# Latent attention with ternary experts: attention moved by a chunk, and the experts' input transposed through DRAM in the last five blocks

## The chip, the cores and the metric

The kernel runs on one core of a Trainium2 chip. The metric is the device time in microseconds (us) of one launch, taken as the median of three runs. One execution was also profiled; its instruction records are the trace that this document reads. The engines are called by their names or as the profile calls them: PE is TensorE (matmuls), PEld its weight loads, DVE is VectorE, ACT is ScalarE, POOL is GpSimd, SP is SyncE, whose queue issues every DMA of this kernel.

## The reference

The input is 4096 tokens of width 512. All is fp32. For each token:

```python
h = layernorm(x)
Q, V = h @ Wq.T + bq, h @ Wv.T + bv           # 16 heads of 32
logits = Q . latent / sqrt(32)                # 64 latent keys per head
w = softmax(top_4(logits))                    # the other 60 weigh nothing
attn = sum(w * latent) + V
x = x + layernorm(attn @ Wo.T + bo)
h = layernorm(x)
up, gate = h @ wu, h @ wg                     # 512 -> 2048, ternary weights
x = x + layernorm((silu(up) * gate) @ wd)     # 2048 -> 512, ternary weights
```

A ternary weight is `clip(round(W / s), -1, 1) * s` with `s = mean(|W|)`. The same latent vectors are keys and values.

## The kernel before

The tokens are cut into 8 blocks of 512 (`NB`, `TB`), a block into 4 row tiles of 128 tokens (`TT`), the width into 4 column tiles (`DC`). Each block goes through attention and then through the experts. The order is written by hand (`manual_schedule`): within one engine, instructions run in the order in which the code emits them, and an instruction waits only for the results and buffers that it needs from other engines, DMAs or its own predecessors.

**The experts** of a block (`class Experts`) run in 16 chunks `e` of 128 hidden columns. A chunk emits `up("u")`, tanh (ACT), `silu` (DVE), `up("g")`, `gate` (DVE), `high` (ACT), `down(e - 1)`, `low` (DVE). Each of `up("u")`, `up("g")` and `down` is 8 matmuls of 128x512, because every activation is split into a high part (rounded to fp32r) and a low part (the rest), and both are multiplied. The PSUM banks of `pu` and `pg` exist once each: `up("u", e + 1)` waits until `silu(e)` has read `pu`, `up("g", e + 1)` until `gate(e)` has read `pg`, and `down(e)`, which is emitted in chunk `e + 1`, needs the high and the low part of chunk `e`. The first matmul of a block reads the high part of all four row tiles, the second the low part.

**The attention** of block b+1 is emitted in pieces between the chunks of block b. The function `pieces` is the list of places: `put(e, k, f, ...)` puts a step into chunk `e` at place `k`. Place 3 is ahead of tanh; place 0 is between tanh and `silu`; place 1 between `up("g")` and `gate`; place 2 behind `down(e - 1)` and ahead of `low`. The steps are, for the attention block `A`:

- `q(c)`: queries of four heads (PE), copied by ACT. `l(c)`: logits (PE), copied by ACT into two tiles `w`. The hidden rows are read as `taken(k)` or `ordered(k)`, two orders of the same transposed tile `hT`.
- `m(i)`, `r(i)`, `e(i)`, `n(i)`, `z(i)` for eight groups of heads: the four largest (DVE), the marking of them (DVE), exponentials (ACT), normalisation (DVE), and a transpose of the weights that is done as a transpose of 32x32 blocks on DVE, a write to DRAM (`dz`), and four loads back (`wT`).
- `v(c)`, `y(c)`: values and the weighted latents in one bank (PE), copied by ACT into `attnT`. The first two `v` use the bank of `pg` (`gate_psum`), the others one of the two banks `at`.
- `o(t)`, `o_bias(t)`: the output projection of a row tile (8 matmul instructions on PE), bias and statistics (DVE). `o_rstd` (POOL), `o_apply(t)`: layer norm (DVE) and the addition to x (POOL).
- `f_stats`, `f_rstd`, `f_apply(t)`: the experts' layer norm; `f_trans(t)`: four transposes of 128x128 on PE into a bank `at`, from which ACT copies the high part `hT_f` and DVE subtracts the low part `lT_f`.

**The next attention block's input** (`after`, two blocks ahead) is loaded by `load_normed` in chunk 6 as four row tiles `xa`, normalised in place (`a_stats`, `a_rstd`, `a_apply`), transposed by `a_blocks` in 32x32 blocks on DVE, one column tile at a time (16 instructions of 128x128), written to DRAM (`da`), and read back by `a_load` into `hT`. `hT` of block b+2 shares its buffer with `hT_f` of block b, so that `a_load` waits for the last gate matmul of the block. Blocks 0 and 1 (`FirstAttention`) and 2 (`SecondAttention`) make `hT` by transposes on PE; block 0's attention is ordered by the string `FIRST_STEPS`.

In before, the places behind the output projection of an attention block are:

```python
put(11, 2, A.o, 0, range(DC), gate_psum)      # and o_bias(0), o(1) to o(3), o_rstd(0, 2)
put(12, 1, A.o_rstd, 2, 4)
put(12, 2, A.o_apply, 0)                      # and 1;  2 and 3 at (13, 0)
put(13, 1, A.f_stats, 0)                      # and 1, f_rstd(0, 2);  2, 3, f_rstd(2, 4) at (13, 2)
put(14, 0, A.f_apply, 0)                      # and 1;  2 and 3 at (14, 1)
put(14, 1, A.f_trans, 0)                      # and 1;  2 and 3 at (15, 0)
```

The functions that the diff touches, and what calls them, with the line numbers of the profile:

Of the kernel before, what the change touches and what calls it, by code (L numbers as in the profile page):

```python
# [10 lines left out]
F32 = mybir.dt.float32  # L11
F32R = mybir.dt.float32r
BF16 = mybir.dt.bfloat16
AF = mybir.ActivationFunctionType
ALU = mybir.AluOpType
AX = mybir.AxisListType

P = 128
# [40 lines left out]
def latent_attention_ternary_glu(  # L59
# [15 lines left out]
    nc = tc.nc  # L75
    NT, D = x_in.shape
    E = wuT.shape[1]
    DC = D // P
    EC = E // P
    TB = 512  # L80
    TT = TB // P
# [5 lines left out]
    work = ctx.enter_context(tc.tile_pool(name="work", bufs=2))  # L87
    small = ctx.enter_context(tc.tile_pool(name="small", bufs=4))
    dram = ctx.enter_context(tc.tile_pool(name="dram", bufs=3, space=bass.MemoryType.DRAM))
# [20 lines left out]
    def transposed(which, b, name, dtype):  # L110
        return work.tile([P, DC, TB], dtype, tag=f"{which}{b % 2}", name=name, bufs=1)
# [7 lines left out]
    CH = E // 2  # L119
    halves = [(k, h) for k in range(DC) for h in range(2)]  # L120
    raw = {}
    late = []
    for q in range(DC):
        w = work.tile([P, D], F32, tag="xa", name=f"raw_d_6_{q}", bufs=TT)
        late.append(w)
    for n, i in RAW_ORDER:
        raw[n, i] = wpool.tile([P, CH], F32, tag="chunk", name=f"raw_{n}_{i}", bufs=6 * DC)
    for q in range(DC):
        raw["d", 6 + q] = late[q]
    count = {"u": 2 * DC, "g": 2 * DC, "d": 2 * DC + 2}  # L130

    def load_x(b):
# [8 lines left out]
    normed = {}  # L141

    def load_normed(b):
        for t in range(TT):
            xt = work.tile([P, D], F32, tag="xa", name=f"xa_{b}_{t}", bufs=TT)
            r = b * TB + t * P
            nc.sync.dma_start(out=xt, in_=x_in[r : r + P, :])
            normed[b, t] = xt

    def load_up(n, src):  # L150
        for i, (k, h) in enumerate(halves):
# [46 lines left out]
    tern = {}  # L198
# [84 lines left out]
    def transpose_row(h, name):  # L283
        pt = at_psum(f"pt_{name}")
        for c in range(DC):
            nc.tensor.transpose(pt[:, c * P : (c + 1) * P], h[:, c * P : (c + 1) * P], ident)  # L286
        return pt.rearrange("p (c k) -> p c k", k=P)
# [3 lines left out]
    class Attention:  # L291
        def __init__(self, b):
            self.b = b
            self.hT = None
            self.attnT = None
            self.norm_a = Norm(f"a{b}")
            self.norm_o = Norm(f"o{b}")
            self.norm_f = Norm(f"f{b}")
            self.rows = {}
            self.qT, self.w, self.top, self.m8, self.left, self.wT, self.pv = ({} for _ in range(7))  # L300
            self.po = {}

        def a_stats(self, t):
            self.norm_a.stats(t, normed[self.b, t])

        def a_rstd(self, lo, hi):
            self.norm_a.rstd(lo, hi)  # L310

        def a_apply(self, t):
            self.norm_a.apply(normed[self.b, t], normed[self.b, t], t)

        def a_blocks(self, c):

            if c == 0:
                self.da = dram.tile([P, 4, DC, P], F32, tag="da", name=f"da_{self.b}", bufs=2)
            z = work.tile([P, 4, P], F32, tag="w", name=f"za_{self.b}_{c}", bufs=4)
            for t in range(TT):  # L320
                nc.vector.transpose(
                    z[:, :, 32 * t : 32 * t + 32],
                    normed[self.b, t][:, c * P : (c + 1) * P].rearrange("p (k j) -> p k j", j=32),
                )
            nc.sync.dma_start(out=self.da[:, :, c, :], in_=z)

        def a_load(self):
            self.hT = transposed("X", self.b, f"hT_{self.b}", F32)
            for k in range(4):
                nc.sync.dma_start(  # L330
                    out=self.hT[32 * k : 32 * k + 32, :, :],
                    in_=self.da.rearrange("(a j) k c e -> k j a (c e)", j=32)[k],
                )

        def taken(self, k):
            return self.hT.rearrange("p a (c e) -> p c a e", e=P)[:, k]

        def ordered(self, k):  # L340
            return self.hT.rearrange("p a (c t i) -> p c t a i", t=TT, i=32)[:, k]


        def q(self, c):
# [145 lines left out]
            self.rows["f", t] = row(f"h_f{self.b}_{t}")  # L490
            self.norm_f.apply(self.rows["f", t], x_tiles[self.b][t], t)

        def f_alloc(self):
            self.hi = transposed("X", self.b, f"hT_f{self.b}", F32R)
            self.lo = transposed("Y", self.b, f"lT_f{self.b}", F32R)

        def f_trans(self, t):
            src = transpose_row(self.rows.pop(("f", t)), f"f{self.b}_{t}")
            dst = self.hi[:, :, t * P : (t + 1) * P]
            nc.scalar.copy(dst, src)  # L500
            nc.vector.tensor_tensor(
                self.lo[:, :, t * P : (t + 1) * P], src, dst.bitcast(F32), ALU.subtract
            )

    class SecondAttention(Attention):
# [9 lines left out]
        def sorted(self, dst, src):  # L517
            return self.mixed(dst), src.rearrange("p (a t i) -> p a t i", t=TT, i=32)

        def a_apply(self, t):  # L520
            self.rows["a", t] = row(f"h_a{self.b}_{t}")
            self.norm_a.apply(self.rows["a", t], normed[self.b, t], t)

        def a_trans(self, t):
            if self.hT is None:
# [143 lines left out]
    class Experts:  # L669
# [6 lines left out]
        def up(self, n, e):  # L676
            p = ps_up.tile([P, TB], F32, tag=n, name=f"p{n}_{self.b}_{e}")
            for k in range(DC):
                for i, part in enumerate(self.parts):
                    nc.tensor.matmul(  # L680
                        p, lhsT=tern[n, 2 * k + e // 8][:, (e % 8) * P : (e % 8 + 1) * P], rhs=part[:, k, :],
                        start=(k == 0 and i == 0), stop=(k == DC - 1 and i == 1),
                    )
            (self.pu if n == "u" else self.pg)[e] = p
# [91 lines left out]
    A = FirstAttention(0)  # L776
# [105 lines left out]
    def pieces(A, after):  # L882

        at = {(e, k): [] for e in range(EC) for k in range(4)}

        def put(e, k, f, *args):
            at[e, k].append(lambda: f(*args))

        if A.b > 1:
            if A.b == 2:  # L890
                put(0, 0, A.a_apply, 0)
                put(0, 0, A.a_apply, 1)
                put(0, 1, A.a_trans, 0)
                put(0, 1, A.a_trans, 1)
                put(0, 1, A.a_apply, 2)
                put(0, 1, A.a_apply, 3)
                put(0, 2, A.a_trans, 2)
                put(0, 2, A.a_trans, 3)
            put(1, 0, A.q, 0)
            put(2, 0, A.q, 1)  # L900
            put(4, 0, A.q, 2)
            put(6, 0, A.q, 3)
        put(1, 1, A.l, 0)
        put(2, 2, A.l, 1)
        for i in range(8):
            put(2 + i, 0, A.m, i)
            put(2 + i, 2, A.r, i)
            put(3 + i, 3, A.e, i)
            put(3 + i, 1, A.n, i)
            put(3 + i, 1, A.z, i)  # L910
        for c in range(2):
            put(5 + 2 * c, 0, A.v, c, gate_psum)
            put(5 + 2 * c, 0, A.y, c)
            put(5 + 2 * c, 0, A.l, c + 2)
        for c in range(2, DC):
            put(5 + 2 * c, 1, A.v, c)
            put(5 + 2 * c, 1, A.y, c)
        if after is not None and after.b == 2:
            put(14, 2, after.a_stats, 0)
            put(14, 2, after.a_stats, 1)  # L920
            put(15, 1, after.a_stats, 2)
            put(15, 1, after.a_stats, 3)
            put(15, 1, after.a_rstd, 0, 4)
        elif after is not None:
            put(10, 2, after.a_stats, 0)
            put(10, 2, after.a_stats, 1)
            put(11, 0, after.a_stats, 2)
            put(11, 0, after.a_stats, 3)
            put(11, 0, after.a_rstd, 0, TT)
            for t in range(TT):  # L930
                put(11, 1, after.a_apply, t)
            for c in range(DC):
                put(11, 2, after.a_blocks, c)
            put(15, 2, after.a_load)
        put(11, 2, A.o, 0, range(DC), gate_psum)
        put(11, 2, A.o_bias, 0)
        for t in range(1, TT):
            put(11, 2, A.o, t)
            put(11, 2, A.o_bias, t)
        put(11, 2, A.o_rstd, 0, 2)  # L940
        put(12, 1, A.o_rstd, 2, 4)
        put(12, 2, A.o_apply, 0)
        put(12, 2, A.o_apply, 1)
        put(13, 0, A.o_apply, 2)
        put(13, 0, A.o_apply, 3)
        put(13, 1, A.f_stats, 0)
        put(13, 1, A.f_stats, 1)
        put(13, 1, A.f_rstd, 0, 2)
        put(13, 2, A.f_stats, 2)
        put(13, 2, A.f_stats, 3)  # L950
        put(13, 2, A.f_rstd, 2, 4)
        put(14, 0, A.f_apply, 0)
        put(14, 0, A.f_apply, 1)
        put(14, 1, A.f_alloc)
        put(14, 1, A.f_trans, 0)
        put(14, 1, A.f_trans, 1)
        put(14, 1, A.f_apply, 2)
        put(14, 1, A.f_apply, 3)
        put(15, 0, A.f_trans, 2)
        put(15, 0, A.f_trans, 3)  # L960
        return at

    prev = None
    for b in range(NB):
        if b > 0:
            A, nxt = nxt, after
        after = None
        F = Experts(b, (A.hi, A.lo))
        at = {}
        for e in range(EC):  # L970
            if e == 4 and 0 < b < NB - 1:
# [119 lines left out]
```

## Time and profile before

| | |
|---|---|
| median of 3 runs | 1169.82 us (1168.61 to 1170.22) |
| profiled execution | 1169.52 us |
| its span, first to last instruction | 1167.3 us |
| PE, DVE, ACT, POOL busy | 1145.6, 853.1, 371.9, 172.7 us |
| granted TensorE clock, mean | 0.998 |
| PE transposes of the experts' input, `pt_f`, 8 blocks | 128 instructions, 17.3 us |
| share of pt_f in the chain that ended last | 1.1% |
| block-transposed weights written to DRAM, `dz` | 56 DMAs, 256 KB each, 2.0 us to landing |
| block-transposed rows written, `da`, and read, `hT` | 20 and 20 DMAs, 256 KB each, 2.9 and 5.1 us to landing |

The time of the profiled execution exceeds its span by 2.2 us, which lie before the first and behind the last recorded instruction. A duration in the profile is that of one instruction; instructions of one engine overlap a little, so the distance from start to start is shorter (a matmul of 128x512 is 390 ns long, and one starts every 227 ns). The chain of waits gives what each stretch of work adds to the end. An instruction's idle time stands in brackets behind it, with what ended it.

### The profile page before, as it was taken

The page shows a single profiled execution, that of the slowest core. Times are in us where ns is not written, and L with a number is a line of the kernel's source. Part 1 is how long each engine was busy: PE and PEld are TensorE (multiplying, and loading weights), DVE is VectorE, ACT ScalarE, POOL GpSimd, SP SyncE. Part 2 cuts the span into 40 slices and gives each one's busy share as a digit, 9 for nine tenths or more (in the row PEclk, how much of TensorE's full clock was granted, in tenths as well). Part 3 has the DMA queues.
Part 4 walks back from the last instruction along what each step waited for, and adds up shares of the span by engine and source line. Part 5 has one row for each costly group of instructions (what it writes and reads, how often), then busy time and mean ns, then how long its engine had stood idle before and what let it go on. Part 6 is the DMA issues. An engine that isn't in the chain of part 4 may idle for free.

```text
span 1167.3 us, 14552 instructions
## 1 busy us (share of the span) xinstructions
PE 1145.6 (98%) x4730; PEld 784.6 (67%) x4730; DVE 853.1 (73%) x2981; ACT 371.9 (32%) x654; POOL 172.7 (15%) x205
## 2 busy tenths in 40 slices
PE   8999999999999999999999999999999999999997
PEld 5446665866757766676766766577665866757885
DVE  5975884968867779777787688776886868847435
ACT  4984441333312332133321232122331233312222
POOL 1066000320023000320003200032000320013100
PEclk9999999999999999999999999999999999999999
DMA  9700121013111231122220232201412112100000
GB/s 353 287 1 1 63 65 54 1 53 129 64 45 37 99 98 56 37 73 75 89 85 6 73 103 78 72 19 54 136 56 63 37 52 93 64 10 1 37 1 36
DMA packets 73323, 80.38 MB, mean 69 GB/s; under 512 B 7200, under 2 KB 46368, under 8 KB 73248
## 3 DMA queue, kind: packets, MB, share of 16 engines
q1 hardware_dynamic: 73248, 79.46, 20.9%
q8 instruction: 37, 0.61, 0.2%
q14 instruction: 38, 0.31, 0.1%
HBM read 51.12 MB, written 28.31 MB: 68 GB/s over the span
## 4 chain that ended last, share of the span: by engine, by line
PE 91%; DVE 6%; ACT 1%; DMA 1%; issue 1%; POOL 0%; SPq 0%; DVEq 0%
PE pg L680 20%; PE pu L680 19%; PE acc L723 19%; PE po L463 8%; PE pv L435 8%; PE pq L348 7%; PE pv L452 3%; PE pl L362 3%; PE pq L553 2%; DVE left L388 1%; PE pt_f L286 1%; DVE m L380 1%; PE po L636 1%; DVE w L408 1%; DVE w L390 0%
## 5 line engine op out<-in xcount | busy, mean ns | idle before, releaser
L680 PE MATMUL pg<-hT_f,tern_g 128*128 128x512 f32 x512 | 211.4, 413 | 0.8 <-ACT attnT L442 0.8
L723 PE MATMUL acc<-tern_d,hi 128*128 128x512 f32 x512 | 202.9, 396 | 1.7 <-DVE y L276 1.7
L680 PE MATMUL pu<-hT_f,tern_u 128*128 128x512 f32 x512 | 203.3, 397 | 0.7 <-ACT hT_f L657 0.7
L723 PE MATMUL acc<-tern_d,lo 128*128 128x512 f32 x512 | 199.8, 390 | 0.1
L680 PE MATMUL pu<-lT_f,tern_u 128*128 128x512 f32 x512 | 199.5, 390 | 0.2 <-DVE lT_f L663 0.2
L680 PE MATMUL pg<-lT_f,tern_g 128*128 128x512 f32 x512 | 199.6, 390 | 0.0
L708 ACT CAST hi<-h 128x512 fp32r<-128x512 f32 x128 | 79.4, 620 | 263.9 <-DVE h L697 263.8
L689 ACT ACTIVATE h<-pu,columns 128x512 f32<-128x512 f32 x128 | 87.2, 681 | 216.1 <-PE pu L680 215.4
L697 DVE TENSOR_TENSOR h<-h,pg 128x512 f32<-128x512 f32 x128 | 86.2, 673 | 85.4 <-PE pg L680 84.7
L692 DVE SCALAR_TENSOR_TENSOR h<-h,pu 128x512 f32<-128x512 f32 x128 | 86.1, 673 | 67.7 <-ACT h L689 67.7
L723 PEld LDWEIGHTS acc<-tern_d,hi 128*128 128x128 f32 x512 | 96.1, 188 | 34.5 <-issue 13.4
L713 DVE TENSOR_TENSOR lo<-h,hi 128x512 fp32r<-128x512 f32 x128 | 93.7, 732 | 34.9 <-ACT hi L708 34.9
L680 PEld LDWEIGHTS pg<-hT_f,tern_g 128*128 128x128 f32 x512 | 96.1, 188 | 27.1 <-issue 4.1
L680 PEld LDWEIGHTS pg<-lT_f,tern_g 128*128 128x128 f32 x512 | 96.2, 188 | 24.3 <-issue 5.7
L680 PEld LDWEIGHTS pu<-hT_f,tern_u 128*128 128x128 f32 x512 | 96.1, 188 | 23.5 <-issue 1.7
L680 PEld LDWEIGHTS pu<-lT_f,tern_u 128*128 128x128 f32 x512 | 96.1, 188 | 21.7 <-issue 1.7
L723 PEld LDWEIGHTS acc<-tern_d,lo 128*128 128x128 f32 x512 | 96.2, 188 | 19.9 <-DVE lo L713 0.9
L435 PE MATMUL pv<-hT,wv 128*128 128x512 f32 x224 | 100.7, 592 | 0.8 <-DVE h L697 0.8
L388 DVE MATCH_REPLACE8 left<-m,w 128x64 f32<-128x64 f32 x512 | 100.3, 211 | 0.0
L463 PE MATMUL po<-wo,attnT 128*128 128x512 f32 x224 | 97.3, 592 | 0.0
L348 PE MATMUL pq<-hT,wq 128*128 128x512 f32 x192 | 86.2, 592 | 0.0
L463 PEld LDWEIGHTS po<-wo,attnT 128*128 128x128 f32 x224 | 42.5, 190 | 50.8 <-issue 48.6
(130 smaller groups left out, 1327.2 us busy)
## 6 DMA issues: line engine op xcount, KB each, us to landing
dz<-z SPq DMA_DIRECT2D x56, 256.0 KB, 2.0
wT<-dz SPq DMA_DIRECT2D x224, 64.0 KB, 1.9
x<-in_x SPq DMA_DIRECT2D x32, 256.0 KB, 3.8
out_x<-x SPq DMA_DIRECT2D x31, 256.0 KB, 2.0
xa<-in_x SPq DMA_DIRECT2D x24, 256.0 KB, 3.5
da<-za SPq DMA_DIRECT2D x20, 256.0 KB, 2.9
hT<-da SPq DMA_DIRECT2D x20, 256.0 KB, 5.1
raw_u<-in_wuT SPq DMA_DIRECT2D x8, 512.0 KB, 8.4
```

What stands on the lines that cost most here:

```text
L348: nc.tensor.matmul(pq, lhsT=wq[:, k, c * P : (c + 1) * P], rhs=self.taken(k), start=(k == 0), stop=(k == DC - 1),)
L362: nc.tensor.matmul(pls[pr][:, t * P : (t + 1) * P], lhsT=qT[rows, t * P : (t + 1) * P], rhs=lk[rows, c, :], start=True, stop=True, tile_po ...
L388: nc.vector.match_replace(left[:, g, :], m8[:, g, :], w[:, g, :], TAKEN)
L435: nc.tensor.matmul(self.pv[c], lhsT=wv[:, k, c * P : (c + 1) * P], rhs=self.ordered(k), start=(k == 0), stop=False,)
L463: nc.tensor.matmul(self.po[t], lhsT=self.attnT[:, c, t * P : (t + 1) * P], rhs=wo[:, c, :], start=(c == 0), stop=(c == DC - 1),)
L680: nc.tensor.matmul(p, lhsT=tern[n, 2 * k + e // 8][:, (e % 8) * P : (e % 8 + 1) * P], rhs=part[:, k, :], start=(k == 0 and i == 0), stop=( ...
L689: nc.scalar.activation(self.h[e], self.pu[e], AF.Tanh, scale=half_u[0])
L692: nc.vector.scalar_tensor_tensor(self.h[e], self.h[e], 1.0, self.pu.pop(e), ALU.add, ALU.mult)
L697: nc.vector.tensor_tensor(self.h[e], self.h[e], self.pg.pop(e), ALU.mult)
L708: nc.scalar.copy(hi, self.h[e])
L713: nc.vector.tensor_tensor(lo, self.h.pop(e), self.hid[e][0].bitcast(F32), ALU.subtract)
L723: nc.tensor.matmul(self.acc[t], lhsT=part[:, t * P : (t + 1) * P], rhs=wd, start=(e == 0 and i == 0), stop=(e == EC - 1 and i == 1),)
```

## The change

Attention blocks 3 to 7 (the five for which `A.b > 2`) get an offset `s = 1`: all their steps from `l` to the output projection move to one chunk earlier, `q` to (0, 2), (1, 1), (3, 0), (5, 0), `m(0)` to (1, 1). Behind the output projection, which is now at (10, 2), the layer norms stand closer together, and `f_trans` gives way to three new steps: `f_blocks(t)` transposes a normalised row tile in 32x32 blocks (one DVE instruction of 128x512) and writes it to DRAM; `f_load(half)` reads two row tiles back with four DMAs; `f_split(t)` copies the high part (ACT) and subtracts the low part (DVE). The tile `whole` that is read back takes the place of the normalised rows `xa`, which become one tile of four row tiles, loaded with one DMA. `a_blocks` now takes one row tile at a time (4 instructions of 128x512 in place of 16 of 128x128), and `taken` and `ordered` read the order that results. For block 1, whose pieces run in block 0, the first two `v` and `y` go to place 1, behind `l`, and into a bank `at`. `f_trans` stays for blocks 1 and 2.

```diff
     def load_normed(b):
-        for t in range(TT):
-            xt = work.tile([P, D], F32, tag="xa", name=f"xa_{b}_{t}", bufs=TT)
-            r = b * TB + t * P
-            nc.sync.dma_start(out=xt, in_=x_in[r : r + P, :])
-            normed[b, t] = xt
+        normed[b] = work.tile([P, TT, D], F32, tag="xa", name=f"xa_{b}", bufs=1)
+        nc.sync.dma_start(
+            out=normed[b], in_=x_in[b * TB : (b + 1) * TB, :].rearrange("(t p) d -> p t d", p=P)
+        )
...
-        def a_blocks(self, c):
...
+        def blocks(self, which, t, h):
+            if t == 0:
+                self.far[which] = dram.tile(
+                    [P, 4, TT, P], F32, tag="far", name=f"far_{which}{self.b}", bufs=3
+                )
+            z = work.tile([P, 4, P], F32, tag="w", name=f"z{which}_{self.b}_{t}", bufs=4)
+            nc.vector.transpose(
+                z.rearrange("p k (c i) -> p c k i", i=32),
+                h.rearrange("p (c k j) -> p c k j", k=4, j=32),
             )
+            nc.sync.dma_start(out=self.far[which][:, :, t, :], in_=z)
+
+        def a_blocks(self, t):
+            self.blocks("a", t, normed[self.b][:, t, :])
...
         def taken(self, k):
-            return self.hT.rearrange("p a (c e) -> p c a e", e=P)[:, k]
+            return self.hT.rearrange("p a (t c i) -> p c a t i", t=TT, i=32)[:, k]
 
         def ordered(self, k):
-            return self.hT.rearrange("p a (c t i) -> p c t a i", t=TT, i=32)[:, k]
+            return self.hT.rearrange("p a (t c i) -> p c t a i", t=TT, i=32)[:, k]
...
+        def f_blocks(self, t):
+            self.blocks("f", t, self.rows.pop(("f", t)))
+
+        def f_load(self, half):
+            if half == 0:
+                self.whole = work.tile([P, 4, TB], F32, tag="xa", name=f"hw_{self.b}", bufs=1)
+            part = slice(2 * half * P, (2 * half + 2) * P)
+            for k in range(4):
+                nc.sync.dma_start(
+                    out=self.whole[32 * k : 32 * k + 32, :, part],
+                    in_=self.far["f"].rearrange("(a j) k t e -> k j a (t e)", j=32)[k][:, :, part],
+                )
+
+        def f_split(self, t):
...
+            src = self.whole[:, :, t * P : (t + 1) * P].rearrange("p a (c i) -> p c a i", i=32)
...
+            nc.scalar.copy(hi, src)
+            nc.vector.tensor_tensor(lo, src, hi.bitcast(F32), ALU.subtract)
...
+        s = 1 if A.b > 2 else 0
...
+        elif A.b > 2:
+            put(0, 2, A.q, 0)
+            put(1, 1, A.q, 1)
+            put(3, 0, A.q, 2)
+            put(5, 0, A.q, 3)
...
         for c in range(2):
-            put(5 + 2 * c, 0, A.v, c, gate_psum)
-            put(5 + 2 * c, 0, A.y, c)
-            put(5 + 2 * c, 0, A.l, c + 2)
+            if A.b > 1:
+                put(5 - s + 2 * c, 0, A.v, c, gate_psum)
+                put(5 - s + 2 * c, 0, A.y, c)
+            put(5 - s + 2 * c, 0, A.l, c + 2)
+            if A.b == 1:
+                put(5 + 2 * c, 1, A.v, c)
+                put(5 + 2 * c, 1, A.y, c)
...
-        put(11, 2, A.o_rstd, 0, 2)
...
+        put(11 - s, 2, A.o_rstd, 0, 2)
+        if s:
+            put(10, 2, A.o_rstd, 2, 4)
+            put(11, 0, A.o_apply, 0)
+            put(11, 0, A.o_apply, 1)
+            put(11, 1, A.o_apply, 2)
+            put(11, 1, A.o_apply, 3)
+            put(11, 2, A.f_stats, 0)
+            put(11, 2, A.f_stats, 1)
+            put(11, 2, A.f_rstd, 0, 2)
+            put(12, 0, A.f_stats, 2)
+            put(12, 0, A.f_stats, 3)
+            put(12, 0, A.f_rstd, 2, 4)
+            for t in range(TT):
+                put(12, 1 + t // 2, A.f_apply, t)
+                put(12, 1 + t // 2, A.f_blocks, t)
+            put(12, 2, A.f_load, 0)
+            put(13, 0, A.f_load, 1)
+            for t in range(TT):
+                put(14 + (t + 2) // 3, (t + 2) % 3, A.f_split, t)
```

## The prediction

> **What bounds the kernel now.** I read the page's busy shares first, then the chain by engine.
>
> ```profile
> PE 1145.6 (98%) x4730; PEld 784.6 (67%) x4730; DVE 853.1 (73%) x2981; ACT 371.9 (32%) x654; POOL 172.7 (15%) x205
> PE 91%; DVE 6%; ACT 1%; DMA 1%; issue 1%; POOL 0%; SPq 0%; DVEq 0%
> ```
>
> TensorE is busy 98% and carries 91% of the chain; VectorE's 73% is an average. A block lasts 140 us (output projections start at 609.15, 749.11, 889.67). So I read the chain in order of time where the change works, behind the output projection (start, length):
>
> ```profile
> 749.11 13.73 PE po L463 x32
> 762.85 1.83 PE pu L680 x8
> 764.67 1.81 PE pg L680 x8
> 766.49 1.81 PE acc L723 x8
> ...
> 777.37 0.87 PE pt_f L286 x8
> 778.25 1.83 PE acc L723 x8
> 780.07 1.82 PE pu L680 x8
> 781.89 0.87 PE pt_f L286 x8
> 782.76 1.84 PE pg L680 x8
> ```
>
> No gap: a chunk is three groups of eight matmuls, 1.815 us each. The projection is already one piece (32 matmuls together), and the transposes are two pieces of 0.87 us. How near VectorE is to TensorE here shows in its timeline:
>
> ```profile
> 764.44 0.66 DVE L713 TENSOR_TENSOR lo<-h,hi 128x512 fp32r<-128x512 f32 x1
> 765.49 0.69 DVE L692 SCALAR_TENSOR_TENSOR h<-h,pu 128x512 f32<-128x512 f32 x1 [0.40 <-ACT h L689]
> 766.52 0.69 DVE L697 TENSOR_TENSOR h<-h,pg 128x512 f32<-128x512 f32 x1 [0.35 <-PE pg L680]
> 767.13 1.00 DVE L276 TENSOR_SCALAR o<-o,mv_o,rs_o 128x512 f32<-128x512 f32 x2
> 768.65 2.95 DVE L276 TENSOR_SCALAR o<-o,mv_o,rs_o 128x512 f32<-128x512 f32 x2
> ...
> 775.91 0.66 DVE L713 TENSOR_TENSOR lo<-h,hi 128x512 fp32r<-128x512 f32 x1
> 776.49 1.00 DVE L276 TENSOR_SCALAR h_f<-x,mv_f,rs_f 128x512 f32<-128x512 f32 x2
> ```
>
> From 764.44 to 776.57 VectorE is idle for 0.40 + 0.35 us only. Its last product there, `lo` of chunk 13, is needed by `down` at 778.25: 1.7 us to spare. Two groups price what is added:
>
> ```profile
> L415 DVE STREAM_TRANSPOSE z<-w 128x512 f32<-128x512 f32 x56 | 39.8, 711 | 1.9
> L276 DVE TENSOR_SCALAR h_f<-x,mv_f,rs_f 128x512 f32<-128x512 f32 x32 | 17.3, 578 | 0.0
> ```
>
> And block 0, chunk 5, has TensorE's real waits:
>
> ```profile
> 126.05 3.70 PE L435 MATMUL pv<-hT,wv 128*128 128x512 f32 x8 [0.84 <-DVE h L697]
> 131.53 1.04 PE L452 MATMUL pv<-wT,lv 128*64 128x512 f32 x2 [0.78 <-DMA wT<-dz]
> 134.47 0.50 PE L680 MATMUL pg<-hT_f,tern_g 128*128 128x512 f32 x1 [0.81 <-ACT attnT L442]
> ```
>
> **Removed from TensorE.** In attention blocks 3 to 7 the 16 transposes go: 2 x 0.87 = 1.74 us per block, all on the path, as the chain shows. Their bank waits go too, at nothing. [...]
>
> **VectorE behind the projection: the term that decides.** Before, the three chunks behind the projection hold four `o_apply`, four statistics and then two `f_apply`; the other two and the splits come later. Now chunks 11 and 12 hold the four `o_apply`, four statistics, four `f_apply` and four block transposes, all ahead of `lo` of chunk 12 in VectorE's queue. Count from the end of the projection. In before, `lo` of chunk 13 ends at 776.57 - 762.85 = 13.72 us, with exactly the work that now stands ahead of the same `lo`, apart from the four new pairs. A pair is `f_apply` 0.54, 0.03 for its result, then the transpose, 0.711 long, with the next instruction 0.07 before its end: 1.21 us. The two idle moments vanish. So `lo` of chunk 12 ends at 13.72 - 0.75 + 4 x 1.21 = 17.81. TensorE wants it for the second matmul of `down(12)`, behind eight groups: 8 x 1.815 + 0.23 = 14.75. It is held up 3.1 us per block, in parts: `gate` frees the pg bank late, `silu` the pu bank, `lo` itself. Queued behind on VectorE are the next `silu` and `gate`; they catch up within chunk 13.
>
> The uncertain size is `o_apply`: 0.5 us alone, 2.95 for two beside GpSimd's x additions; three blocks of before show 2.95, three 1.97. The new order meets the additions in the same way (`o_apply` 2 is queued 0.6 us behind the start of the first addition), so I take 2.95 and keep 2.1 us as the low end of the delay. At the other end `f_apply` can be held by GpSimd's rstd pair (longest h_f 1.32 against a median of 0.54): +0.8, 3.9 us. [...]
>
> **The end of the block.** Split 3 now stands behind `high(15)` on ScalarE; before, all splits ended 1.8 us ahead of the next block's first matmul (784.47 against 786.26). With E the end of gate group 15, `up(15)` ends at E-1.81. ScalarE: tanh, cast of split 1, cast of split 2 (0.58, 0.53, 0.62) end E+0.0. VectorE: `silu` from E-1.0, `lo` 1 from E-0.4, `lo` 2 from E+0.2, `gate` from E+0.76 (not E+0.03), done E+1.44. Then the `high` cast (0.53 to the next start) and the cast of split 3 done E+2.6, `lo` 3 done E+3.3. TensorE arrives at E+1.81 behind `down(14)`, waits 0.85 for the high part, one matmul later 0.46 for the low part: 1.3 us per block (1.0 to 1.9, as no row has this cast with 32-element runs).
>
> **The DRAM path.** SP's queue is empty in before from 751.2 until the hT load at 784.45, which waits for TensorE anyway, so four writes and eight loads per block delay nobody. Landing: the last block transpose ends at 17.15; its write lands 2.9 us later (row da), 20.1. Half 0 is issued by 19.4 and lands by 21.3 (row wT, 1.9) to 24.5 (row hT, 5.1); its first reader stands at 24.4. Half 1 is issued by 21.8, lands at 23.7 to 26.9, and is wanted at 27.9. Covered, with 1.0 us left at the worst; without that cover each microsecond costs one per block, since split 2 stands ahead of `high(15)`.
>
> **Edits at nothing.** `load_normed` as one 1 MB transfer is issued three chunks (over 16 us) ahead of its reader; a 1 MB load took 7.9 us at the crowded start (wq). The a-blocks change from 16 x 0.2 us to four of 0.71 us, under the projection, where VectorE waits 1.9 us. The strides of `taken` and `ordered` change, but reads in runs of 128 elements (pq, L348) and of 32 (pv, L435) have a mean of 592 ns both. Attention a chunk earlier: `q(0)` wants hT, issued at the last gate group (5.1 us to land) and read four groups later (7.2 us). VectorE's cycle per group of heads is 7.66 us (122.40 to 130.07) in the new order too; `y_out` now meets `m(0)` and `r(0)`, but that chunk has `q(1)` and `l(0)`, 10 us of TensorE against about 9. The wait of `y(0)` for wT eases: gaps from `v(0)` to the gate group of 5.78, 5.54, 5.61, 6.20, 5.65 against 5.53 undisturbed, 0.2 us per block gained.
>
> **Block 0.** `v(0)` goes behind `l(2)` and `up("g")` into another bank: the three waits above (0.84, 0.78, 0.81) are covered, one more fp32 switch costs 0.2. I take -2.5 us (0 to -2.9).
>
> **Sum.** Per block -1.74 - 0.2 + 3.1 + 1.3 = +2.45; five blocks +12.3; block 0 -2.5: +9.8. The profiled execution took 1169.52 us (span 1167.3 and 2.2 around it), the median of the runs is 1169.82. Forecast 1179.6. Ends per block: -1.94 + 2.1 + 1.0 = +1.2 and -1.74 + 3.9 + 1.9 = +4.1; with block 0's ends +3 to +20.
>
> **Rivals.**
> - Faster: the VectorE work fits. If TensorE's 14.75 us covered the queue and the splits were in time, only the removals are left: 5 x -1.94 - 2.5 = -12.2, 1157.6. For it: 98% TensorE and 73% VectorE. Against: 17.81 us of queue, 13.72 of it measured. It decides from 3 us of VectorE time less per block and a gate at E. Chance 0.07.
> - No change: `o_apply` free of GpSimd (four at 0.5) takes 1.96 us off each delay: per block +0.5, in all 1170. For it: the two at 1.00. Against: no steady block has all four so. Chance 0.12.
> - The round trip lands late: loads at 5.1 us plus 3 more would hold split 2, `high(15)` and the next block by 2 us: 5 x 2 more, 1189.6. For it: the margin of 1.0. Against: a half moves half of what the 5.1 us row moves. Chance 0.14.
> - The projection "in one piece" is worth nothing, since it was one: that part does not do what its name says, whichever case holds.
>
> **How the numbers follow.** The forecast has 0.67. The range, 1173 to 1188, takes in its ends but for the extremes. A measurement of this kernel can tell about 0.2%, 2.3 us, from no change. Slower 0.87 (forecast, late landing, upper part of the third case), same 0.06, faster 0.07.
>
> **What would show it.** Right: TensorE idle in chunks 11 to 13 of five blocks, released by `h` (L727, L722) and `lo` (L743), about 3 us; a wait of the first pu matmul of a block on hT_f and lT_f of 1.3 us; the block period 142.4 instead of 140; chunk 5 of block 0 without waits. Wrong: a period under 139; VectorE idle before `lo` of chunk 12; casts waiting for hw.

## The result, and the profile after

The change makes the kernel slower: 1187.47 us median of 4 runs (1186.56 to 1188.89), against 1170.02 us for the kernel before on the same chip (1168.61 to 1171.39). The ratio is 1.0157, interval 1.0143 to 1.0171: about 17.5 us where 9.8 were forecast. The profiled execution took 1186.56 us, its span is 1184.8 us (17.5 more than before), and the mean granted clock is 0.995 instead of 0.998.

The page of the kernel after, busy shares and chain by engine:

```profile
PE 1146.2 (97%) x4650; PEld 775.2 (65%) x4650; DVE 859.8 (73%) x2941; ACT 371.5 (31%) x654; POOL 168.6 (14%) x205
PE 80%; DVE 14%; ACT 2%; issue 2%; DMA 1%; POOL 0%; SPq 0%; DVEq 0%; ACTq 0%
```

TensorE has 80 instructions fewer and is busy 0.6 us longer. The busy shares hardly move, but VectorE's share of the chain goes from 6% to 14%: TensorE now waits for VectorE in places. Which places, the view of TensorE's waits in the kernel after tells (us in total, how often, the longest):

```profile
PE pu L710 <- ACT hT_f L517: 7.1, 5, 1.4
PE pg L710 <- DVE h L727: 4.2, 5, 0.8
PE acc L753 <- DVE lo L743: 3.1, 5, 0.6
PE pv L436 <- ACT w L371: 2.1, 1, 2.1
...
PE pu L710 <- DVE h L722: 1.5, 5, 0.3
```

The lines with a count of 5 come once per changed block: three behind the projection (`gate`, `lo`, `silu`), and the high part of the next block's input, `hT_f`, with a smaller one for `lT_f` (1.2 us in all) behind it. `v(0)` in block 0 waits once for 2.1 us (fourth line), and the first `q(0)` that reads its `hT` from DRAM once for 0.8 us. None is for the landing of `hw`: ScalarE's casts were never idle for it.

The chain of the kernel after in order of time, for the same block as the prediction showed (start, length):

```profile
752.05 13.75 PE po L464 x32
...
782.50 0.58 DVE lo L743
783.12 1.88 PE acc L753 x7
785.01 1.81 PE pu L710 x8
...
793.59 0.07 DVE lT_f L518
...
794.20 0.68 DVE h L722
...
795.40 0.69 DVE h L727
...
796.73 0.53 ACT hT_f L517
...
797.28 0.70 DVE lT_f L518
...
798.02 1.88 PE pu L710 x7
799.91 1.81 PE pg L710 x8
```

Two detours off TensorE: one that ends with `lo` of chunk 12, one with the last split. Between the starts of the projections (608.88, 752.05, 895.21, 1038.38) lie 143.17, 143.16 and 143.17 us; in before they were 139.96, 140.56 and 140.08, and the forecast was 142.4.

Subtracting the starts of the projections, corrected by the chunk of 5.44 us that they moved forward, distributes the 17.5 us: -0.5 at the start of the execution, ahead of the first projection, 0.8 at the first `q(0)`, then 4.9, 3.2, 2.6, 3.1 and 3.4 in the five changed blocks. The 4.9 holds something of its own. The matmuls of the kernel after at the end of that first block:

```profile
510.08 0.68 PE L710 MATMUL pu<-lT_f,tern_u 128*128 128x512 f32 x1 [0.23 <-DVE lT_f L518]
510.55 0.63 PE L710 MATMUL pu<-hT_f,tern_u 128*128 128x512 f32 x1
```

They stand behind the wait for `hT_f` (1.41 us), one matmul and the wait for `lT_f`. From here until 513.5 a matmul starts every 0.43 us, against 0.227 in the same groups elsewhere: the granted clock was lower for 3.4 us (0.52 over 510.1 to 513.5). The other four ends of blocks show the same waits and no such stretch. This cost 1.6 us once: the period that holds it is 144.77 us, the others 143.17.

### The profile page after: what moved, and what is told of

It is laid out like the page before. It is cut to its first block, busy times and chain, and to the rows that moved or that the text cites. A ratio compares the mean times of both kernels' runs of the same rounds, so it can differ in the third digit from the quotient of the medians.

```text
span 1184.8 us, 14426 instructions
## 1 busy us (share of the span) xinstructions
PE 1146.2 (97%) x4650; PEld 775.2 (65%) x4650; DVE 859.8 (73%) x2941; ACT 371.5 (31%) x654; POOL 168.6 (14%) x205
## 4 chain that ended last, share of the span: by engine, by line
PE 80%; DVE 14%; ACT 2%; issue 2%; DMA 1%; POOL 0%; SPq 0%; DVEq 0%; ACTq 0%
PE pu L710 16%; PE acc L753 16%; PE pg L710 16%; PE pv L436 8%; PE po L464 8%; PE pq L349 7%; PE pv L453 2%; PE pl L363 2%; PE pq L583 2%; DVE left L389 1%; DVE h L727 1%; DVE o L272 1%; DVE st_f L245 1%; DVE h L722 1%; DVE lo L743 1%
## 5 line engine op out<-in xcount | busy, mean ns | idle before, releaser
L710 PE MATMUL pu<-hT_f,tern_u 128*128 128x512 f32 x512 | 206.6, 404 | 9.3 <-ACT hT_f L517 7.1
L710 PE MATMUL pg<-hT_f,tern_g 128*128 128x512 f32 x512 | 209.0, 408 | 4.2 <-DVE h L727 4.2
L743 DVE TENSOR_TENSOR lo<-h,hi 128x512 fp32r<-128x512 f32 x128 | 90.7, 708 | 24.3 <-ACT hi L738 24.3
```

The costliest lines, as they stand in the source:

```text
L710: nc.tensor.matmul(p, lhsT=tern[n, 2 * k + e // 8][:, (e % 8) * P : (e % 8 + 1) * P], rhs=part[:, k], start=(k == 0 and i == 0), stop=(k = ...
L743: nc.vector.tensor_tensor(lo, self.h.pop(e), self.hid[e][0].bitcast(F32), ALU.subtract)
```

## Experiments

The theory, which the trace of after suggested: the loss has separate causes, (1) VectorE's queue behind the projection, which I read as 2.6 us per block, (2) the order of splits, `silu` and `gate` at the end of the block, which I read as 1.9 us per block, (3) a wait in block 0 that eats the gain there, and (4) drops of the clock behind long waits. Rivals: the loss comes with moving the attention forward as such; or with the DRAM round trip. The edits of places are in `pieces`.

**Splits earlier (e1).** Two splits in (14, 2), two in (15, 0), so that all are ahead of `silu(15)`, `gate(15)` and `high(15)` on their engines.

```diff
-                put(14 + (t + 2) // 3, (t + 2) % 3, A.f_split, t)
+                put(14 + t // 2, 2 - 2 * (t // 2), A.f_split, t)
```

> The changed kernel with the four splits of a block at (14, 2), (14, 2), (15, 0), (15, 0) in place of (14, 2), (15, 0), (15, 1), (15, 2). Theory (order on ScalarE and VectorE): split 3 no longer stands behind high(15), so the wait of 1.9 us at the first matmuls of a block goes in five blocks, -9.5; but then q(0) is reached as early as in the one block of the changed kernel without that wait, where it waited 0.8 us for hT: +3.2 to +4. About 1181. Rival (the rows come back from DRAM late): ScalarE waits for the loads in front of the earlier casts, and the time is 1187 or more.

Measured: 1174.02 us, ratio 1.0038 (1.0028 to 1.0049), ten runs. The chain of this kernel over a block's end:

```profile
744.84 13.75 PE po L464 x32
...
786.86 1.81 PE acc L753 x8
788.67 1.81 PE pu L710 x8
790.49 1.81 PE pg L710 x8
792.30 1.81 PE acc L753 x8
794.11 3.61 PE pq L349 x8
```

Nothing stands between TensorE's groups any more, so the rows were back from DRAM in time for the earlier casts too. The first `pg` of the next block starts 45.65 us behind the projection's start (790.49 - 744.84); in after it was 47.86 (799.91 - 752.05). So cause 2 is shown, with its size: 2.2 us per block, more than I had read. The period falls by less, from 143.17 to 141.2 us, because `q(0)` now comes so early that it is held a little (3.61 us for its eight matmuls instead of 3.43 in after). The waits behind the projection stay (4.1, 3.0 and 1.5 us in all). The expectation of 1181 was too high: it had put 3.2 to 4 us on waits of `q(0)`, and only the first `q(0)` waits for long (0.55 us). The span is 13.4 us shorter than that of after: 10 by the period, 1.6 by the drop of the clock that went with the wait, and 1.75 ahead of the first changed block, in work that the edit does not touch. Nearly all of that last part is another drop of the clock, behind `v(0)` in block 0, which the profile of after has and that of e1 has not (below).

**`o_apply` on ScalarE (e2).** In the five blocks VectorE only computes the shift (0.11 us each), and ScalarE normalises.

```diff
-            self.norm_o.apply(o, o, t)
+            if self.b > 2:
+                self.norm_o.shift(t)
+                self.norm_o.apply_scalar(o, o, t)
+            else:
+                self.norm_o.apply(o, o, t)
```

> The changed kernel with the normalisation in o_apply of blocks 3 to 7 done on ScalarE, with a small product on VectorE per row tile. Theory (VectorE's queue behind the output projection): about 3.5 us leave that queue and 0.9 come, lo of chunk 12 is ready 1.2 to 2.6 us earlier (the statistics may then wait for GpSimd's additions), and five blocks give -6 to -13: 1175 to 1181. Rival (the block transposes and the way through DRAM hold TensorE, whatever stands ahead of them): no change, 1187.

Measured: 1186.78 us, 1.0142 (1.0117 to 1.0167): no different from after. The expectation fell. VectorE's timeline of this kernel shows one reason:

```profile
768.93 0.69 DVE L245 BATCH_NORM_STATS2 st_f<-x 128x6 f32<-128x512 f32 x1 [0.36 <-POOL x L484]
```

The statistics now come so early that three of them wait for GpSimd's additions, 0.35 us and more each, and the four pairs of `f_apply` and transpose are still ahead of `lo` of chunk 12. It ends 0.96 us sooner, where 1.2 to 2.6 were expected; over five blocks that is 4.8 us. The other reason: behind the unchanged wait for `hT_f` the clock fell in four of the five blocks here (seven matmuls of `pu` took 3.14, 1.88, 2.52, 2.94 and 3.32 us; 1.88 is the one at full clock), mean clock 0.990. The period is 142.20 us where the clock held and 143.81 where it fell, so that a drop costs 1.6 us: 6.4 in four blocks, 1.6 in after. The 4.8 us won at the one place are the 4.8 lost at the other. Why four here and one in after, with waits of the same length, stays open; e3 and e4 have the same waits and no drop behind any of the ten.

**Block 0: three places.** e3 is after with the first two `v` and `y` of block 1 put back to place 0 and the bank of `pg`. e5 is before with only the change's move. e4 is after with them at place 2, behind `down`; e10 is before with them there.

```diff
 # e3, from after
-            if A.b > 1:
-                put(5 - s + 2 * c, 0, A.v, c, gate_psum)
-                put(5 - s + 2 * c, 0, A.y, c)
+            put(5 - s + 2 * c, 0, A.v, c, gate_psum)
+            put(5 - s + 2 * c, 0, A.y, c)
             put(5 - s + 2 * c, 0, A.l, c + 2)
-            if A.b == 1:
-                put(5 + 2 * c, 1, A.v, c)
-                put(5 + 2 * c, 1, A.y, c)
 # e4, from after
-                put(5 + 2 * c, 1, A.v, c)
-                put(5 + 2 * c, 1, A.y, c)
+                put(5 + 2 * c, 2, A.v, c)
+                put(5 + 2 * c, 2, A.y, c)
 # e5, from before (e10 the same with place 2 in the last two lines)
-            put(5 + 2 * c, 0, A.v, c, gate_psum)
-            put(5 + 2 * c, 0, A.y, c)
+            if A.b > 1:
+                put(5 + 2 * c, 0, A.v, c, gate_psum)
+                put(5 + 2 * c, 0, A.y, c)
             put(5 + 2 * c, 0, A.l, c + 2)
+            if A.b == 1:
+                put(5 + 2 * c, 1, A.v, c)
+                put(5 + 2 * c, 1, A.y, c)
```

> The changed kernel with the first two v and y of block 1 back at place 0 and in the bank of pg, as in before. Theory: in block 0 the new wait of v(0) for a bank, 2.15 us, and the lower clock behind it have eaten all that the move gained, so undoing it changes nothing: 1187, within 1. Rival (the move gained the 2.5 us that were forecast and the rest of the change lost them): 1190.

> The kernel before with only the move of the first two v and y of block 1 behind l and into a bank at. Theory (bank wait and clock): 1169.8, within 1 of before. Rival (the forecast): 1167.3.

> The changed kernel with the first two v and y of block 1 at place 2, behind down(e - 1), still in a bank at. Theory: the 1.8 us of down cover most of the wait of v(0) for the bank, and the lower clock behind it does not come: -2 to -4, 1183 to 1185. Rival (ScalarE is late by more than that, behind two casts of ternary weights): no change.

> The kernel before with only the first two v and y of block 1 moved to place 2, behind down(e - 1), and into a bank at. Theory: the three waits of block 0 (0.84, 0.78, 0.81 us) go and no new wait and no lower clock comes: 1166 to 1167. Rival (VectorE or ScalarE bounds block 0 anyway): 1169.

| | from | us | ratio to before |
|---|---|---|---|
| e3, move undone | after | 1187.96 | 1.0153 (1.0129 to 1.0177) |
| e5, move alone | before | 1168.47 | 0.9991 (0.9980 to 1.0001) |
| e4, place 2 | after | 1182.26 | 1.0113 (1.0094 to 1.0132) |
| e10, place 2 alone | before | 1164.80 | 0.9965 (0.9951 to 0.9978) |

As it was built, the move is worth nothing that can be measured, in either kernel (e3 and e5 came as expected, e4 and e10 0.7 and 1.2 us faster). Why, the timeline of after shows (ScalarE, then TensorE):

```profile
126.03 2.19 ACT L233 ACTIVATE tern_g<-raw_g,columns 128x1024 fp32r<-128x1024 f32 x2
...
129.33 1.06 ACT L371 ACTIVATE w<-pl 128x512 f32<-128x512 f32 x2
129.97 5.40 PE L436 MATMUL pv<-hT,wv 128*128 128x512 f32 x8 [2.15 <-ACT w L371]
```

`v(0)` left the bank of `pg` and its three waits (0.84, 0.78, 0.81), but the bank `at` that it takes holds the logits `pl` until ScalarE has copied them, and this copy is queued behind two casts of the ternary gate weights, 2.19 us. One wait of 2.15 us took the place of three. The clock fell behind it too: over the 5.40 us of these `v`, windows of the trace give (PE, PEld, DVE, ACT, POOL busy, granted clock, DMA share, GB/s)

```profile
130.00:135.40 5.40, 5.40 (x10) 2.09 (x12) 5.26 (x25) 0.40 (x1) 0.00 (x0) 0.68 0.17 60
```

a clock of 0.68, and eight matmuls that take 3.59 us in the timeline of e4 took 5.40. This drop does not come in every execution: the profiles of after, e2, e5 and e6 have it, those of e1 and e7, with the same wait (2.13 us), have not. Where it stays away, the stretch from chunk 5 to the next projection is 1.6 to 1.7 us shorter than in before, so that the move alone is worth that much, and the drop takes it back. At place 2 the copy has another group of eight matmuls (`down`) in which to run, and the chain of e10 is

```profile
128.61 1.90 PE acc L723 x7
130.52 3.43 PE pv L435 x8
```

no wait ahead of `v`, and eight of its matmuls in 3.43 us; `down` itself waits 0.45 us for `lo`. From the first projection to the second it takes 144.91 us, against 148.45 in before and 148.47 in e5. In before that is worth 0.35%, 3.7 us, the only single edit of this study that clearly beats before. It is more than the 2.43 us of the three waits that went, and more than the expected 1166 to 1167: a wait costs TensorE some 0.3 us more than its idle time (in the chain of e9 the group of eight behind one takes 2.11 us, an undisturbed group 1.81), since the matmuls behind it start further apart at first (in after 783.12 and then 783.46, instead of 0.227 us later), and the overlap of two matmuls (390 ns long, one every 227) is lost.

**The attention forward, nothing else (e6).** After with the layer norms spread as in before (each a chunk earlier) and `f_trans` on PE; no experts' input through DRAM.

```diff
-                put(12, 1 + t // 2, A.f_apply, t)
-                put(12, 1 + t // 2, A.f_blocks, t)
...
+            put(13, 0, A.f_apply, 0)
...
+            put(13, 1, A.f_trans, 0)
...
+            put(14, 0, A.f_trans, 3)
```

> The changed kernel with only the attention a chunk forward in the last five blocks: the layer norms and the transposes on TensorE stand behind the output projection as in before, each a chunk earlier, and nothing goes through DRAM for the experts. Theory (the queue on VectorE and the late splits cost the time, moving the attention forward costs nothing but a wait of q(0) for hT): 1169 to 1173. Rival (the attention a chunk forward itself costs, by y_out and the first groups of heads meeting in chunk 1): over 1176.

Measured: 1170.44 us, 1.0007 (0.9998 to 1.0017). TensorE has no wait behind a projection or at the end of a block, only the first `q(0)` waits for `hT` (0.6 us), and the period is 140.3. Moving the attention forward costs nothing: this rival falls.

**The pairs in two chunks (e7).** `f_apply` and `f_blocks` of rows 0 and 1 in (12, 2), of 2 and 3 in (13, 2), each half loaded behind its pair, splits in (14, 2) and (15, 1).

```diff
-                put(12, 1 + t // 2, A.f_apply, t)
-                put(12, 1 + t // 2, A.f_blocks, t)
-            put(12, 2, A.f_load, 0)
-            put(13, 0, A.f_load, 1)
+                put(12 + t // 2, 2, A.f_apply, t)
+                put(12 + t // 2, 2, A.f_blocks, t)
+                if t % 2:
+                    put(12 + t // 2, 2, A.f_load, t // 2)
             for t in range(TT):
-                put(14 + (t + 2) // 3, (t + 2) % 3, A.f_split, t)
+                put(14 + t // 2, 2 - t // 2, A.f_split, t)
```

> The changed kernel with f_apply and f_blocks of tiles 0 and 1 at (12, 2) and of 2 and 3 at (13, 2), f_load behind each pair, and the splits at (14, 2) twice and (15, 1) twice. Theory (VectorE's queue): gate(12) and lo(12) come 2.4 us earlier, so the 2.6 us behind the projection fall to 0.3, but the last rows now land about 26.7 us behind the projection, so that about 1.2 us of waiting stay at the end of a block: 139.9 us per block, 1170 to 1173. Rival (round trip through DRAM): the landing is later than that and each block waits 3 us or more at its end, 1180 or more.

Measured: 1172.19 us, 1.0025 (1.0010 to 1.0039). The waits for `gate` and `lo` are gone from the list; what is left is 1.5 for `silu`, 2.9 for `hT_f` and 1.5 for `lT_f` in all, periods 139.9 to 141.0. So cause 1 is where the pairs stand, ahead of one `lo`. Spread over two chunks, VectorE's work nearly fits: 0.8 us per block stay behind the projection (30.90 us from its start to the first group of chunk 14, where e8 below needs 30.06).

**All repairs together (e8), and the last pairs sooner (e11).** e8 is e7 with e2's `o_apply` and e4's place. e11 is e8 with rows 2 and 3 at (13, 1) instead of (13, 2), load behind them.

```diff
 # e8, from after: the edits of e2, e4 and e7
 # e11, from e8
-                put(12 + t // 2, 2, A.f_apply, t)       # f_blocks and f_load likewise
+                put(12 + t // 2, 2 - t // 2, A.f_apply, t)
```

> The changed kernel with the pairs later (f_apply and f_blocks at (12, 2) and (13, 2), splits at (14, 2) twice and (15, 1) twice), the normalisation of o_apply on ScalarE, and the first two v and y of block 1 at place 2. Theory (VectorE's queue, the order of the splits and the bank wait are the whole cost; without them the removed transposes show): lo of chunk 12 is in time, the last rows land about 25.7 us behind the projection, just in time; 138.4 to 139.2 us per block in place of 139.95, 4 to 7 us in five blocks, and 3 to 4 in block 0: 1160 to 1163. Rival (GpSimd's additions or the landing take the place of VectorE's queue): 1166 or more.

> The reworked kernel (pairs later, o_apply on ScalarE, block 1's first v and y at place 2) with f_apply and f_blocks of tiles 2 and 3 at (13, 1), ahead of gate(13), in place of (13, 2). Theory (what is left at the end of a block is the landing of the last rows, 1.4 us): the write starts 0.6 us sooner, gate(13) is still in time, and each of five blocks gains 0.6: 1160 to 1162. Rival (gate(13) comes late and gives it back): 1163.6 or more.

e8: 1163.64 us, 0.9956 (0.9943 to 0.9968): faster than both kernels, just above the expected 1160 to 1163. Most of this is block 0: beside e10's 0.9965 on the same chip the reworked DRAM path is 1.2 us better than the transposes on PE by the medians, and the intervals overlap. Behind the projection nothing waits any more:

```profile
739.94 13.73 PE po L464 x32
...
770.00 1.83 PE pu L714 x8
```

From the projection's start to the first group of chunk 14 it takes 30.06 us, and in after 32.96 (785.01 - 752.05). So cause 1 cost 2.9 us per block, more than the 2.6 that I had read. A line of the chain of before gives the size of the removal:

```profile
786.42 1.81 PE pu L680 x8
```

This group, the first of the next block, starts 37.31 us behind the projection (786.42 - 749.11), and twelve groups and the 16 transposes stand between. Without transposes the projection and twelve groups take 30.06 + 3 x 1.815 = 35.50: 1.8 us less (1.8 to 1.9 in the other blocks). The chain of e8 also shows where part of this stays:

```profile
773.48 2.95 DMA far_f<-zf
...
777.79 2.86 DMA hw<-far_f
```

The round trip of the last rows is now the late one, and the first matmul of the next block waits up to 1.1 us for it. e11 was to give it time and did not: 1165.95 us, 0.9976 (0.9965 to 0.9987), not told apart from e8, where 1160 to 1162 were expected. In the second changed block, whose projection starts at 601.16 in e11 and at 601.11 in e8, VectorE finished the last block transpose at 632.04 instead of 632.76. SyncE's queue of e11:

```profile
627.34 1.69 SPq L323 DMA_DIRECT2D far_f<-zf  x2
631.11 1.74 SPq L507 DMA_DIRECT2D hw<-far_f  x4
632.94 1.20 SPq L323 DMA_DIRECT2D far_f<-zf  x2
```

The writes of rows 2 and 3 were not issued until 632.94, since the loads of the first half stand ahead of them in the queue and wait for the writes of rows 0 and 1 to land (2.9 us in the median of the writes here). In e8 they were issued from 632.87. The 0.7 us gained on VectorE was nothing at the queue. In the first changed block the writes of rows 0 and 1 landed later in e11, and those of rows 2 and 3 were issued 33.57 us behind the start of the projection instead of 31.99.

**What a wait does to the clock (e9, e12).** Before, with 7 (e9) or 9 (e12) more statistics on VectorE ahead of `gate(15)` in the five blocks; their results are not used.

```diff
+            for j in range(7):                # 9 in e12
+                put(15, 1, A.extra, j)
...
+        def extra(self, j):
+            st = small.tile([P, 6], F32, tag="st", name=f"st_extra{self.b}_{j}")
+            nc.vector.bn_stats(st, x_tiles[self.b][j % TT])
```

> The kernel before with seven more statistics of VectorE, whose results are not used, ahead of gate(15) in each of the five steady blocks. They hold gate(15) by 4.9 us, 2.9 of which the next groups cover: a wait of about 2 us of TensorE per block. Theory (a wait is followed by a lower granted clock for about 3 us, in most but not all executions): 10 us for the waits and up to 10 for the clock, 1182 to 1190, with a granted clock under 0.9 in windows behind the waits. Rival (a wait costs its length): 1180 and a clock of 1.00 there.

> The kernel before with nine statistics of VectorE, whose results are not used, ahead of gate(15) in each of the five steady blocks; with seven, TensorE waited 1.65 us per block and kept its clock. Theory (a longer gap can be followed by a lower clock): a wait of 2.85 us per block, 14 us in all, and in some of the blocks up to 1.6 us more, 1183 to 1191, with a mean granted clock of 0.990 to 0.995. Rival (the clock does not answer to gaps in TensorE's work): 1183 and 0.998.

e9: 1177.93 us, 1.0072 (1.0057 to 1.0087), below both expectations, with waits of 1.62 to 1.65 us in five blocks and a clock of 0.998 in all four executions: no drop. e12: 1186.95 us, 1.0170 (1.0151 to 1.0189), waits of 2.81 to 2.84 us, clocks 0.995, 0.995, 0.992 and 0.989. Two more statistics of 0.59 us in five blocks are 5.9 us, but the medians rose by 18.1 where e9's rose by 8.4, 9.7 more; the rest goes with the lower clocks. The chains of e9 and of e12 behind the same wait:

```profile
650.64 2.11 PE pg L684 x8
```

```profile
654.12 3.43 PE pg L684 x8
```

In e12 this happened in two of five blocks of the profiled execution (3.43 and 3.19 us, the others 2.11); in e9 in none.

## Why the prediction was right and wrong

- **Direction and main mechanism: right.** VectorE's queue behind the projection holds TensorE up. The lines of after:

```profile
769.46 2.56 DVE L272 TENSOR_SCALAR o<-o,mv_o,rs_o 128x512 f32<-128x512 f32 x2
...
777.66 0.71 DVE L319 STREAM_TRANSPOSE zf<-h_f 128x512 f32<-128x512 f32 x1
...
782.42 0.65 DVE L743 TENSOR_TENSOR lo<-h,hi 128x512 fp32r<-128x512 f32 x1
```

  The end of `lo` of chunk 12 was forecast 17.81 us behind the projection and came at 17.27 (783.07 - 765.80); a pair costs 1.2 us as counted. The difference is mostly the pair of `o_apply` beside GpSimd, 2.56 us instead of the 2.95 that I chose. The second matmul of `down` started at 17.32, 2.6 us behind the 14.75 that I counted; but in e8, where nothing holds it, it starts at 14.6, and with what the waits cost beyond their idle time the term is 2.9 us (e8 above) where 3.1 were forecast. No `f_apply` was held here (0.50 to 0.54 us), so the 0.8 of the other end did not come. Nor does before show GpSimd's rstd pair holding one: its `h_f` of 1.32 us ran beside an operation of GpSimd on weights (L230, 1.12 us from 89.30), and two that ran beside an rstd pair took 0.52 and 0.54 us.
- **Removed transposes: right.** They gave 1.8 to 1.9 us per block, 1.74 forecast. The 0.2 us for `y(0)` came too: from the first matmul of `v(0)` to the gate group it takes 5.62 us in all five blocks of after, and 5.62 to 6.28, 5.84 in the mean, in before.
- **The end of the block: the step failed in its order.** I wrote "VectorE: `silu` from E-1.0, `lo` 1 from E-0.4, `lo` 2 from E+0.2, `gate` from E+0.76". Place 0 lies between tanh and `silu`, so the subtraction of split 1 is emitted ahead of `silu`, and it waits there 1.72 us for its cast, which ScalarE does behind tanh. `silu` stands behind a wait that belongs to a split:

```profile
793.59 0.69 DVE L518 TENSOR_TENSOR lT_f<-hw,hT_f 128x512 fp32r<-128x512 f32 x1 [1.72 <-ACT hT_f L517]
```

  With E at 794.1, `lo` 1 ran at E-0.5, `silu` at E+0.1 and `gate` at E+1.3. The term is 2.2 us (e1) instead of 1.3, beyond the 1.9 of the range given. The order makes 0.5 of the 0.9 that are missing, since `gate` came that much later than forecast. The rest is that TensorE was at the next block's first matmul 0.2 us sooner than E+1.81 (the last matmul of `down` started at 795.50), and that a wait costs more than its idle time. e1 takes all of it away by the place alone.
- **Block 0: the step failed.** That "the three waits above (0.84, 0.78, 0.81) are covered" came true, but I priced the new bank at nothing and did not ask what frees it: the copy of the logits on ScalarE, behind the ternary casts. -2.5 became 0 (e3, e5), which was the end of the range and not the value, and part of that is the drop of the clock behind the new wait. What the idea was worth, e10 shows: 3.7 us, one place further. The 0.2 for a switch can be seen in the chain of before: eight `pg` matmuls right behind `pl` take 2.04 us, the next groups 1.81.
- **The clock: no step at all.** Every wait was priced by its length. Where the clock fell behind one, it cost 1.3 to 1.7 us more.
- **`q(0)` and `hT`:** put down at nothing with 7.2 us for 5.1; the first one waited 0.8 us, the other four did not.
- **DRAM path: right.** All landed in time in after (2.6 us for a write of `far_f`, 3.3 us for a load of `hw`, in the median). The rival that priced late landing at 1189.6 lies near the measured time by another cause; its mechanism appears only in e7, e8 and e11, where the last rows come later.
- **The faster rival** asked for 3 us of VectorE time less per block and a gate in time. e8 did that, by places and by ScalarE, and got below before, though most of that is block 0.

By my own steps with the measured sizes, a block is -1.85 - 0.2 + 2.9 + 2.2 = +3.05, and the periods show +3.0 (143.17 against 140.2 in the mean). Five are +15.2. With 0 for block 0, 1.6 for the clock, 0.8 for `hT` and the -0.5 at the start of the execution that is 17.1 of 17.5. So the 7.7 us above the forecast are mostly the end of the block (4.5), block 0 (2.5) and the clock, and VectorE's smaller term took 1 us back. That the total still lies inside the range given, near its upper end, owes something to luck: the range had no place for the clock.

## What to carry to other kernels

A step that is "at nothing" must be asked who frees its buffer, and what stands ahead of that one on its engine: in block 0 a bank that looked free was held by a copy queued behind casts (2.15 us of waiting), and in e11 writes that were ready stood 0.9 us behind loads in SyncE's queue. Place work that waits for another engine behind the products that TensorE wants next, not ahead of them; the same 1.2 us pairs cost 2.9 us a block in one chunk and 0.8 in two. Price a wait of TensorE by more than its idle time: some 0.3 us each time here, and 1.3 to 1.7 us more where the clock fell behind it. It fell, in some profiles, behind waits of 1.67 to 2.84 us, and behind some of 1.41 us with one of 0.23 us after them.

## What the hardware showed

The clock of TensorE fell behind some gaps in these runs, and not behind others of the same length. The profiles of the 14 kernels hold, among others, these waits (idle time of TensorE, and behind how many of them the clock fell):

| idle | where | drops |
|---|---|---|
| 1.41 and 0.23 us, one matmul between | end of a block: after, e2, e3, e4 | 1, 4, 0 and 0 of 5 each |
| 1.62 to 1.65 us | e9 | 0 of 5 |
| 1.67 to 1.68 us | last block of every kernel, `down` waits for `y` | 3 of 14 (e2, e5, e10) |
| 2.10 to 2.15 us | block 0: after, e1, e2, e5, e6, e7 | 4 of 6 |
| 1.87 and 2.35 us, each with 0.31 behind one matmul | end of a block: e11 | 0 of 2 |
| 2.81 to 2.84 us | e12 | 2 of 5 |

The shortest wait of a single piece with a drop behind it, in e10 (the second line is a window, in the order given above):

```profile
1073.14 0.47 PE L723 MATMUL acc<-tern_d,hi 128*128 128x512 f32 x1 [1.68 <-DVE y L276]
1074.50:1078.00 3.50, 3.50 (x8) 2.75 (x9) 2.19 (x3) 0.62 (x1) 3.50 (x3) 0.51 0.48 183
```

So the length of the wait alone did not tell here whether the clock fell: behind 1.41 us it fell in four of five blocks of e2 and in none of e3 and e4. Behind a drop one matmul of these groups started every 0.43 us instead of 0.227, for some 3.4 us (in after from 510.1 to 513.5 at a clock of 0.52, in e10 for 3.50 us at 0.51). Why equal gaps differ, no run here shows.
